# Graph attention's encoder on TensorE: exponentials as weights instead of values as weights

## The chip, the cores and the metric

The kernel runs on one core of a Trainium2 chip. A core has a matrix engine (TensorE: PE for its matmuls, PEld for its weight loads), VectorE (DVE), ScalarE (ACT), GpSimd (POOL) and SyncE (SP); the last two mostly issue transfers (DMAs). The matrix engine writes its results into eight PSUM banks, each of 512 float32 columns on 128 partitions. Everything else is held in SBUF or in the chip's main memory. The metric is the time of one whole execution in microseconds (us).

## What is computed

A stack of four graph layers on 2708 nodes with 512 features. The change lies in the first of them, an attention with 4 heads of 128 features each. The scores are a sigmoid of a sum of two numbers, one per target node and one per source node, and each head's weights are a softmax over a node's neighbours:

```python
Xw = einsum('hnd,hde->hne', Xh, W)
f1 = einsum('hnd,hd->hn', Xw, V[:, 0, :, 0])
f2 = einsum('hnd,hd->hn', Xw, V[:, 1, :, 0])
sig = sigmoid(f1[:, :, None] + f2[:, None, :])
att = softmax(where(adj != 0, adj * sig, -inf), axis=-1)
Xa = einsum('hij,hjd->hid', att, Xw)          # the encoder's attention
Xn = batchnorm(Xa); emb = batchnorm(elu(Xn @ We.T + be) + Xn)
Y = einsum('hij,hjd->hid', att, emb)          # the decoder's attention
```

Both patterns that the layer is given are the same matrix, so both softmaxes are one. After this layer come a graph convolution and two attention layers over the same matrix; the change doesn't touch them.

## The kernel before

The attention runs as a pass over parts. A part is one half of the target nodes (`hf`, 1354 nodes each) for two heads (`p`, heads 2p and 2p+1), in the order hf 0 p 0, hf 0 p 1, hf 1 p 0, hf 1 p 1. Within a part the loop at L465 goes over 22 blocks of source nodes, 21 of 128 and one of 20 (`ORDER` puts the short one in the middle).

For each block `form` (L367) makes the exponentials t, [source nodes, 2 heads, 1354 targets]:

- A load of the adjacency's block (`a`, four buffers) comes through SP's queue. In parts with p = 0 (`prepare`) VectorE turns its zeros into a large negative number (L396, L397), and GpSimd stores the result to `adj_d`. The parts with p = 1 read `adj_d` back.
- ScalarE takes a tanh for each head (L408), VectorE multiplies both by the block (L416), ScalarE takes the exponential of both (L417). t has four buffers.
- Some blocks' t (`kept_d`, 4 of a p = 0 part, 8 of a p = 1 part) are stored by GpSimd for the decoder (L486).

TensorE then multiplies (L504): the weights are the values `xw` of the block, 128 features of a head, and the exponentials stream through, 452 or 450 targets at a time. A part's results stand in six banks as [features, targets]: two heads by three chunks. A float32 matmul appears in the trace as two passes, each with its weight load.

The softmax's denominators are made by separate matmuls (L541): weights of 32 columns of ones, 340 targets at a time, four chunks in four column groups of the array, into the two banks `psm0` and `psm1`. In parts with p = 1 two neighbouring blocks are added on VectorE first (L531), so that one such set serves both; the first three and the last two blocks of a part stand alone.

At a part's end `keep` (L621) copies the six banks to `ft`, the features by nodes, on VectorE and ScalarE by turns. The denominators go to memory, come back spread over 80 partitions, are inverted there, go to memory again, and are loaded as a row on all partitions (`rb`). Results of the part are multiplied by it and counted for the batch norm (`bn_stats`) between the next part's blocks, one piece at a time from a list `later`. The last part does it at once with a matmul that spreads the reciprocals (L680). The decoder uses the reciprocals too, from `rs_d` in memory (`spread_sums`).

The order of each engine's instructions comes from a scheduler that places them by priorities and by its own times; each engine then works its list strictly in order. Waits between engines are semaphores. With the change, too, the order is fixed before the run.

Of the kernel before, what the change touches and what calls it, by code (L numbers as in the profile page):

```python
# [17 lines left out]
P = 128  # L18
# [11 lines left out]
def gnn_stack_kernel(  # L30
# [47 lines left out]
    ones = const.tile([P, P], F32, name="ones")  # L78
# [13 lines left out]
    def rows_tile(name):  # L92
        return big.tile([P, NT, F], F32, tag="rows", name=name)
# [52 lines left out]
    SQ = 4  # L146
    SW = 2 * ((HW + 2 * SQ - 1) // (2 * SQ))
    SCH = [[(q * SW, min(SW, w - q * SW)) for q in range(SQ)] for _, w in HSPAN]

# [8 lines left out]
    ALONE, LAST = 3, 2  # L158
    assert ORDER.index(NT - 1) % 2 == ALONE % 2 == NT % 2 + 1
# [18 lines left out]
    with ExitStack() as l0:  # L178
# [10 lines left out]
        SR = SQ * SW // 17  # L189
        assert SR <= P and SR * 17 == SQ * SW  # L190
        sum_d = dram.tile([H, NHALF, SQ, SW], F32, name="sum_d")
        rs_d = dram.tile([H, NHALF, SQ, SW], F32, name="rs_d")
# [4 lines left out]
        ones32 = p0.tile([P, 32], F32, name="ones32")  # L197
        nc.vector.memset(ones32, 1.0)
# [12 lines left out]
        xw = rows_tile("xw")  # L211
# [7 lines left out]
        def project(att, psum):  # L219
# [61 lines left out]
            def values_of(jt):  # L281
# [3 lines left out]
                for h in range(H):  # L285
# [10 lines left out]
                    xw[:n, jt, :].rearrange("p (a k d) -> p a k d", a=H // HP, k=HP),  # L296
# [13 lines left out]
            def rest(step):  # L310

                with tc.issue_after(step.ins):
# [7 lines left out]
                    copies(xw[:, NT - 1, :])  # L320
# [5 lines left out]
        def spread_sums(att, hf, p):  # L326

            w = HSPAN[hf][1]
            t = att.tile([P, HP, HW], F32, tag="rb", name="rb", bufs=1)
            src = rs_d[HP * p : HP * (p + 1), hf]  # L330
            even = (SQ - 1) * SW
            for k in range(HP):
                nc.sync.dma_start(
                    t[:, k, :even],
                    src[k, : SQ - 1].rearrange("r w -> (r w)").partition_broadcast(P),
                )
                nc.sync.dma_start(
                    t[:, k, even:w],
                    src[k, SQ - 1, SW - (w - even) :].partition_broadcast(P),
                )  # L340
            return t

        def attention_pass(values, first, att, psum, finish, f1b=None, blocks=(), spread=None, rest=None, taken={}):
# [84 lines left out]
            def sum_tiles():  # L428
                return [
                    psum.tile([P, BANK], F32, tag=f"psm{k}", name="psm", bufs=1) for k in range(HP)  # L430
                ]
# [4 lines left out]
            po = None  # L436
            for hf, (h0, w) in enumerate(HSPAN):
                for p in range(H // HP):
# [22 lines left out]
                    sums = None  # L461
                    if first and rest is None:
                        sums = sum_tiles()
                    before = None
                    for place, jt in enumerate(ORDER):  # L465
# [8 lines left out]
                        if kept is None or first:  # L474
# [6 lines left out]
                            if rest is not None:  # L481
                                rest(step)
                                rest = None
                                sums = sum_tiles()
# [7 lines left out]
                        if po is None:  # L492
# [6 lines left out]
                            po = [both[q][:, k, :] for k in range(HP) for q in range(HB)]  # L499
                        for k in range(HP):  # L500
# [10 lines left out]
                        if not first:  # L511
                            continue


                        if prepare or not ALONE <= place < NT - LAST:
                            whole, m = [t[:, k, :] for k in range(HP)], n
                        elif n < P:
                            m = P
                            for k in range(HP):
                                nc.vector.tensor_tensor(  # L520
                                    whole[k][:n, :w], whole[k][:n, :w], tv[:, k, :], ALU.add
                                )
                        elif before is None:
                            before = t
                            continue
                        else:

                            whole, m = [], P
                            for k, tag in enumerate(("z", "pair")):
                                both = att.tile([P, HW], F32, tag=tag, name="pair", bufs=1)  # L530
                                nc.vector.tensor_tensor(  # L531
                                    both[:, :w], before[:, k, :w], tv[:, k, :], ALU.add
                                )
                                whole.append(both)
                            before = None
                            if BLOCKS[ORDER[place + 1]][1] < P:
                                continue
                        for k in range(HP):
                            for r, (q0, qw) in enumerate(SCH[hf]):

                                nc.tensor.matmul(  # L541
                                    sums[k][32 * r : 32 * r + 32, :SW],
                                    ones32[:m],
                                    whole[k][:m, q0 + qw - SW : q0 + qw],
                                    start=(place == 0),
                                    stop=(place == NT - 1),
                                )
                    later += finish(hf, p, po, sums if first else rb) or []
# [20 lines left out]
        def stats_tile(name, k):  # L569
            return p0.tile([P, C, k, 6], F32, tag=name, name=name)  # L570
# [39 lines left out]
        stats = stats_tile("stats_a", SQ * NHALF)  # L610
        bias = p0.tile([P, 2, C], F32, name="enc_bias")
        with (
# [8 lines left out]
            def keep(hf, p, po, sums):  # L621
# [3 lines left out]
                final = hf == NHALF - 1 and p == H // HP - 1  # L625
                for k in range(HP):
                    for q, (q0, qw) in enumerate(HCH[hf]):
                        copy = nc.scalar.copy if q % 2 else nc.vector.tensor_copy
                        taken[q % 2] = copy(
                            ft[:, HP * p + k, h0 + q0 : h0 + q0 + qw], po[HB * k + q][:, :qw]  # L630
                        )
                sm = [att.tile([P, BW], F32, tag="rs", name="sm") for _ in range(HP)]
                if not final:
                    for k in range(HP):
                        h = HP * p + k
                        nc.vector.tensor_scalar(
                            sm[k][:, :SW], sums[k][:, :SW], TINY, None, ALU.max
                        )
                        nc.gpsimd.dma_start(sum_d[h, hf], sm[k][0 : 32 * SQ : 32, :SW])
                    part = slice(HP * p, HP * (p + 1)), hf  # L640
                    few = att.tile([SR, HP, 17], F32, tag="few", name="few", bufs=1)
                    wide = "h r w -> h (r w)"
                    cut = "h (s e) -> s h e"
                    nc.sync.dma_start(few, sum_d[part].rearrange(wide).rearrange(cut, s=SR))
                    nc.vector.reciprocal(few, few)
                    nc.sync.dma_start(rs_d[part].rearrange(wide).rearrange(cut, s=SR), few)
# [1423 lines left out]
```

## Time and profile before

| | us |
|---|---|
| median of 3 runs | 3197.55 (3196.16 to 3198.11) |
| the profiled execution's own time | 3195.56 |
| its span, first to last instruction | 3193.5 |
| encoder's attention, first to last matmul | 39.2 to 536.9 |
| granted TensorE clock, mean of the span | 0.997 |

In the four parts of the encoder's attention, and in the stage after it up to the encoder's MLP, the engines were busy as follows (us, instructions in brackets):

```profile
39.00:169.70 130.70, 130.12 (x621) 55.99 (x617) 119.09 (x73) 114.44 (x70) 18.11 (x32) 1.00 0.79 276
169.70:287.30 117.60, 116.58 (x474) 52.91 (x474) 104.68 (x66) 109.97 (x68) 6.24 (x11) 1.00 0.71 243
287.30:419.40 132.10, 131.13 (x617) 56.58 (x617) 122.08 (x88) 115.97 (x70) 15.21 (x27) 0.99 0.79 278
419.40:536.90 117.50, 116.56 (x476) 52.81 (x472) 96.45 (x68) 100.79 (x62) 4.95 (x9) 1.00 0.58 203
536.90:571.20 34.30, 31.34 (x109) 14.22 (x109) 25.93 (x41) 22.18 (x24) 5.59 (x8) 1.00 0.62 224
```

The columns are: the window and its length, then busy time of PE, PEld, DVE, ACT and POOL, the granted clock as a share of full speed, the mean busy share of the DMA engines, and what they moved in GB/s. Busy time counts each instruction to its end, although the next one on the same engine often starts a little earlier; the period from start to start is what tells how fast a sequence can go.

### The profile page before, as it was taken

What the parts mean: (1) busy time and instruction counts of PE and PEld (TensorE: products, weight loads), DVE (VectorE), ACT (ScalarE), POOL (GpSimd) and SP (SyncE); (2) the same over time, 40 slices, a digit from 0 to 9 for tenths busy, and PEclk for the clock granted to TensorE, in tenths of its full rate; (3) what the DMA queues carried; (4) which work ended last, traced back from release to release, by engine and by line L of the source; (5) the groups of instructions that cost most, each with busy time, mean ns of one, the idle gap of its engine ahead of it and who ended that gap; (6) DMA issues with size and microseconds to landing.
All of it is one profiled execution on the core that took longest, in us unless ns stands there. A gap on an engine that the chain in (4) does not pass through costs nothing.

```text
span 3193.5 us, 36039 instructions
## 1 busy us (share of the span) xinstructions
PE 3145.5 (98%) x13400; PEld 2125.6 (67%) x13400; DVE 2102.4 (66%) x3746; ACT 1356.7 (42%) x1623; POOL 202.7 (6%) x296
## 2 busy tenths in 40 slices
PE   8999999999999999999999999999999999999999
PEld 5444444544444446885578787777678888888886
DVE  7889987777686684444267667777644555555565
ACT  6899896477867552001133333434301111111111
POOL 1100100000000000000011111120110000000000
PEclk9999999999999999999999999999999999999999
DMA  7867875146555413541154445556431111111111
GB/s 274 314 223 251 284 246 188 65 155 236 173 167 199 172 61 98 144 125 43 40 149 138 140 143 150 154 174 177 132 102 36 52 50 49 49 52 50 49 45 34
DMA packets 207301, 429.81 MB, mean 135 GB/s; under 512 B 21966, under 2 KB 137474, under 8 KB 201302
## 3 DMA queue, kind: packets, MB, share of 16 engines
q1 hardware_dynamic: 183390, 324.15, 33.4%
q0 software_dynamic: 23296, 101.26, 8.5%
q8 instruction: 105, 1.72, 0.2%
q10 hardware_dynamic: 440, 2.10, 0.2%
q14 instruction: 70, 0.57, 0.1%
HBM read 330.07 MB, written 95.90 MB: 133 GB/s over the span
## 4 chain that ended last, share of the span: by engine, by line
PE 85%; DVE 6%; issue 3%; ACT 3%; DMA 2%; POOL 0%; SPq 0%; DVEq 0%; ACTq 0%; POOLq 0%
PE po L504 22%; PE po L1546 18%; PE ps_s L1342 17%; PE ps_nb L1156 7%; PE ps_wide L1206 5%; PE psm L541 3%; PE ps_sup L1734 2%; PE ps_mlp L792 2%; PE ps_hid L128 2%; PE ps_dec L923 2%; PE ps_v L128 1%; DVE t L416 1%; ACT t L408 1%; ACT t L417 1%; DVE e L1832 1%
## 5 line engine op out<-in xcount | busy, mean ns | idle before, releaser
L416 DVE SCALAR_TENSOR_TENSOR t<-t,a 128x2708 f32<-128x2708 f32 (+1 forms) x152 | 450.2, 2975 | 144.3 <-ACT t L408 140.3
L408 ACT ACTIVATE t<-f1b,f2h 128x1354 f32<-128x1354 f32 (+1 forms) x304 | 416.2, 1412 | 45.4 <-PE po L504 35.1
L417 ACT ACTIVATE t<-t 128x2708 f32<-128x2708 f32 (+1 forms) x152 | 373.1, 2456 | 98.8 <-DVE t L416 98.6
L504 PE MATMUL po<-t,xw 128*128 128x452 f32 (+3 forms) x1056 | 409.1, 551 | 3.5 <-ACT t L417 2.9
L1342 PE MATMUL ps_s<-q,hT 128*128 128x256 f32 (+1 forms) x1848 | 405.5, 372 | 0.0
L504 PE MATMUL po<-t,emb 128*128 128x452 f32 (+3 forms) x1056 | 397.6, 545 | 4.0 <-ACT t L417 3.8
L1546 PE MATMUL po<-sup,e 128*128 128x256 f32 (+1 forms) x1512 | 396.9, 384 | 3.1 <-DVE c L1627 2.1
L1342 PEld LDWEIGHTS ps_s<-q,hT 128*128 128x128 f32 x1848 | 339.2, 190 | 49.5 <-issue 6.4
L504 PEld LDWEIGHTS po<-t,xw 128*128 128x128 f32 (+1 forms) x1056 | 189.0, 190 | 211.8 <-issue 194.7
L504 PEld LDWEIGHTS po<-t,emb 128*128 128x128 f32 (+1 forms) x1056 | 193.5, 190 | 201.3 <-issue 190.8
L1546 PEld LDWEIGHTS po<-sup,e 128*128 128x128 f32 (+1 forms) x1512 | 264.2, 185 | 59.3 <-issue 21.5
L1546 PE MATMUL po<-held,T 128*128 128x256 f32 x1200 | 294.8, 380 | 4.8 <-DVE T L1503 4.8
L1546 PEld LDWEIGHTS po<-held,T 128*128 128x128 f32 x1200 | 226.3, 190 | 38.9 <-DVE T L1503 7.6
L1922 DVE SCALAR_TENSOR_TENSOR e<-a_cols,ps_s 128x512 f32<-128x512 f32 (+1 forms) x121 | 79.9, 660 | 238.1 <-PE ps_s L1342 231.9
L1342 PE MATMUL ps_s<-hT 128*128 128x256 f32 (+2 forms) x968 | 217.0, 375 | 4.3 <-DVE e L1832 3.4
L1342 PEld LDWEIGHTS ps_s<-hT 128*128 128x128 f32 x968 | 176.2, 192 | 32.7 <-DVE e L1832 3.8
L1828 ACT ACTIVATE a_score<-a_score,neg_big 128x512 f32<-128x512 f32 (+2 forms) x131 | 88.9, 686 | 256.6 <-DMA a_score<-in_adjT_dram 108.1
L1156 PE MATMUL ps_nb<-hid_hi,at 128*128 128x512 f32 x484 | 185.5, 390 | 0.4 <-DVE at L1148 0.4
L1156 PE MATMUL ps_nb<-hid_lo,at 128*128 128x512 f32 x462 | 180.0, 390 | 0.0
L1452 ACT ACTIVATE e<-e 128x512 f32<-128x512 f32 (+1 forms) x187 | 113.6, 617 | 133.2 <-DVE e L1451 130.1
L1914 ACT ACTIVATE q<-ps_wide,uq 128x256 f32<-128x256 f32 (+1 forms) x44 | 20.5, 467 | 337.1 <-PE ps_wide L1206 337.1
L1503 DVE TENSOR_TENSOR T<-e 128x256 f32<-128x256 f32 x200 | 84.2, 421 | 120.2 <-PE po L1546 97.1
(283 smaller groups left out, 4091.1 us busy)
## 6 DMA issues: line engine op xcount, KB each, us to landing
a<-adj_d SPq DMA_DIRECT2D x108, 677.0 KB
a_cols<-in_adjT_dram SPq DMA_DIRECT2D x200, 256.0 KB
a<-in_adjT_dram SPq DMA_DIRECT2D x42, 677.0 KB
adj_d<-a POOLq DMA_DIRECT2D x42, 677.0 KB, 5.3
kept<-t POOLq DMA_DIRECT2D x20, 1354.0 KB, 6.1
t<-kept SPq DMA_DIRECT2D x20, 1354.0 KB
raw<-in_adjT_dram SPq DMA_DIRECT2D x105, 256.0 KB
a_score<-in_adjT_dram SPq DMA_DIRECT2D x55, 256.0 KB
```

The costliest lines, as they stand in the source:

```text
L128: nc.tensor.matmul(ps[:n], xt[:, c, :n], w[:, c, :], start=(c == 0), stop=(c == C - 1))
L408: tanh = nc.scalar.activation(tv[:, k, :], f1b[k][:n, :w], AF.Tanh, bias=f2h[:n, jt, h : h + 1], scale=0.5,)
L416: step = nc.vector.scalar_tensor_tensor(tv, tv, GUARD, ab, ALU.add, ALU.mult)
L417: exp = nc.scalar.activation(tv, tv, AF.Exp, scale=0.5)
L504: nc.tensor.matmul(po[HB * k + q][:, :qw], values[r : r + n, jt, h * P : (h + 1) * P], t[r : r + n, k, q0 : q0 + qw], start=(place == 0), ...
L541: nc.tensor.matmul(sums[k][32 * r : 32 * r + 32, :SW], ones32[:m], whole[k][:m, q0 + qw - SW : q0 + qw], start=(place == 0), stop=(place = ...
L1156: nc.tensor.matmul(pos[it][:n], at, half[:, jt, :], start=(jt == 0 and k == 0), stop=(jt == NT - 1),)
L1206: nc.tensor.matmul(ps[:, :width], w(c, o), xt(c), start=(c == 0), stop=(c == C - 1),)
L1342: nc.tensor.matmul(ps[:, jb, i:w], keys[:, c, j : j + P], st["q"][:, c, i:], start=(c == 0), stop=(c == C - 1),)
L1452: nc.scalar.activation(e, e, AF.Exp)
L1546: nc.tensor.matmul(po[bank][rows, half, :], lhsT, rhs, start=(k == 0 and half == 0) if first is None else first, stop=last, skip_group_che ...
L1828: nc.scalar.activation(a, a, AF.Identity, bias=neg_big[: a.shape[0]], scale=1.0e30)
```

## The change

In the encoder's attention the roles of the two operands are exchanged. A block of exponentials, 128 sources by 128 targets, is loaded as weights, and the values stream through it, 128 features and a column of ones: 129 columns. The result is [targets, features], with the denominator in its last column. A half has 11 groups of targets (10 of 128 and one of 74). Three results of 129 columns fit a bank, so each of the two heads takes four banks, and all eight are in use. The matmuls of `ones` and the pair sums are no longer there.

At a part's end VectorE takes each group's denominators (maximum with a tiny number, reciprocal) and multiplies the results out of PSUM into `rows`. TensorE turns `rows` back to [features, targets] by transposes, into banks of the part's second head, and VectorE copies these to `ft`. This (`turn`) is issued during the next part's first two blocks, one head in each; the second head's matmuls of these two blocks are held back (`waiting`) until then. The reciprocals are turned as well and stored to `rs_d`. The decoder's pass keeps its form, and reads the reciprocals as one row.

```diff
-    ones = const.tile([P, P], F32, name="ones")
+    ones = const.tile([P, 1], F32, name="ones")
...
+    VW = F + H
...
-        xw = rows_tile("xw")
+        xw = rows_tile("xw", VW).rearrange("p t (h e) -> p t h e", h=H)
+        nc.vector.memset(xw[:, :, :, P:], 1.0)
...
-            for k in range(HP):
-                nc.sync.dma_start(
-                    t[:, k, :even],
-                    src[k, : SQ - 1].rearrange("r w -> (r w)").partition_broadcast(P),
-                )
-                nc.sync.dma_start(
-                    t[:, k, even:w],
-                    src[k, SQ - 1, SW - (w - even) :].partition_broadcast(P),
-                )
+            for k in range(HP):
+                nc.sync.dma_start(
+                    t[:, k, :w], rs_d[HP * p + k, h0 : h0 + w].partition_broadcast(P)
+                )
...
+            def node_sums(k, place, jt, t, w, hf):
+                n = BLOCKS[jt][1]
+                slots = list(range(NB))
+                if n < P:
+                    slots.sort(key=lambda r: r % PER)
+                for r in slots:
+                    b, s = divmod(r, PER)
+                    i0, m = NODES[hf][r]
+                    own = 0 if n == P else b % HB * Q
+                    nc.tensor.matmul(
+                        po[k][b][:m, s * DR : (s + 1) * DR],
+                        t[own : own + n, k, i0 : i0 + m],
+                        values[own : own + n, jt, HP * pair + k, :],
+                        start=(place == 0 and s == 0),
+                        stop=(place == NT - 1),
+                        skip_group_check=True,
+                    )
...
+                        if first:
+                            node_sums(0, place, jt, t, w, hf)
+                            waiting.append(lambda a=(1, place, jt, t, w, hf): node_sums(*a))
+                            if turns:
+                                turns.pop(0)()
+                            if not turns:
+                                for work in waiting:
+                                    work()
+                                waiting = []
+                            continue
...
-                        if prepare or not ALONE <= place < NT - LAST:
-                            whole, m = [t[:, k, :] for k in range(HP)], n
...
-                                nc.tensor.matmul(
-                                    sums[k][32 * r : 32 * r + 32, :SW],
-                                    ones32[:m],
-                                    whole[k][:m, q0 + qw - SW : q0 + qw],
-                                    start=(place == 0),
-                                    stop=(place == NT - 1),
-                                )
...
-            def keep(hf, p, po, sums):
+            def keep(hf, p, po, later):
...
+                for k in range(HP):
+                    rc = att.tile([P, NB], F32, tag="rc", name="rc", bufs=4)
+                    nc.vector.memset(rc[:, NB - 1 :], 1.0)
+                    rows = att.tile([P, NB, P], F32, tag="rows", name="rows")
...
+                    for b, g in groups:
+                        m = NODES[hf][g[0]][1]
+                        src = po[k][b][:m, g[0] % PER * DR : (g[-1] % PER + 1) * DR]
+                        src = src.rearrange("p (r e) -> p r e", e=DR)
+                        own = rc[:m, g[0] : g[-1] + 1]
+                        nc.vector.tensor_scalar(own, src[:, :, P], TINY, None, ALU.max)
+                        nc.vector.reciprocal(own, own)
+                        taken[k] = nc.vector.tensor_tensor(
+                            rows[:m, g[0] : g[-1] + 1, :],
+                            src[:, :, :P],
+                            own.unsqueeze(2).to_broadcast([m, len(g), P]),
+                            ALU.mult,
+                        )
...
+                def turn(k):
+                    h = HP * p + k
+                    rows, rc = kept[k]
+                    for b in range(TURNS):
+                        slots = range(b * QUAD, min(NB, (b + 1) * QUAD))
+                        bank = po[1][(TURNS * k + b) % (HB + 1)]
+                        for r in slots:
+                            i0, m = NODES[hf][r]
+                            nc.tensor.transpose(
+                                bank[:, r % QUAD * P : r % QUAD * P + m],
+                                rows[:m, r, :],
+                                ident[:m, :m],
+                            )
...
+                        if b + 1 == TURNS:
+                            nc.tensor.transpose(bank[:NB, BANK - P :], rc, ident)
+                            sm = att.tile([NB, P], F32, tag="sm", name="sm")
+                            nc.vector.tensor_copy(sm, bank[:NB, BANK - P :])
...
+                        nc.vector.tensor_copy(dst, bank[:, :cw])
+                        later.append(
+                            lambda dst=dst, n=TURNS * hf + b: nc.vector.bn_stats(
+                                stats[:, h, n, :], dst
+                            )
+                        )
...
-                    nc.tensor.matmul(pm, ones, w1_held[:, c, :], start=(c == 0), stop=(c == C - 1))
+                    nc.tensor.matmul(pm, ones.to_broadcast([P, P]), w1_held[:, c, :], start=(c == 0), stop=(c == C - 1))
```

## The prediction

> **What bounds the kernel now.** I read the page first (busy shares and the chain), then the busy time by stage inside the encoder's attention, then the timelines of VectorE, ScalarE and TensorE there.
>
> ```profile
> span 3193.5 us, 36039 instructions
> PE 3145.5 (98%) x13400; PEld 2125.6 (67%) x13400; DVE 2102.4 (66%) x3746; ACT 1356.7 (42%) x1623; POOL 202.7 (6%) x296
> ...
> PE po L504 22%; PE po L1546 18%; PE ps_s L1342 17%; PE ps_nb L1156 7%; PE ps_wide L1206 5%; PE psm L541 3%; PE ps_sup L1734 2%; PE ps_mlp L792 2%; PE ps_hid L128 2%; PE ps_dec L923 2%; PE ps_v L128 1%; DVE t L416 1%; ACT t L408 1%; ACT t L417 1%; DVE e L1832 1%
> ```
>
> The chain runs along TensorE. Only the encoder's half of L504 and all of L541 (the sums, 3%) belong to this change.
>
> ```profile
> core 0: us, PE busy (x) PEld busy (x) DVE busy (x) ACT busy (x) POOL busy (x), PEclk, DMA share, GB/s
> 109.00:170.00 61.00, 61.00 (x289) 26.44 (x282) 51.42 (x33) 52.27 (x33) 6.42 (x11) 1.00 0.82 288
> 437.00:530.00 93.00, 92.07 (x360) 42.27 (x356) 81.66 (x57) 82.94 (x50) 3.77 (x7) 1.00 0.61 217
> ```
>
> TensorE is full in both kinds of part, but VectorE and ScalarE stand at 84 to 89%. A gain on TensorE is soon capped, so I need the period of each engine for one block of 128 sources.
>
> The chain of waits, in order of time (start, us; two blocks of the first part), and then the timelines of VectorE and ScalarE there:
>
> ```profile
> 115.45 4.75 PE po L504 x12
> 121.48 4.75 PE po L504 x12
> ```
>
> ```profile
> 62.42 2.98 DVE L416 SCALAR_TENSOR_TENSOR t<-t,a 128x2708 f32<-128x2708 f32 x1
> 65.32 0.86 DVE L396 TENSOR_SCALAR z<-a 128x1354 f32<-128x1354 f32 x1
> 66.22 1.57 DVE L397 SCALAR_TENSOR_TENSOR a<-z,a 128x1354 f32<-128x1354 f32 x1
> 67.92 2.98 DVE L416 SCALAR_TENSOR_TENSOR t<-t,a 128x2708 f32<-128x2708 f32 x1
> ```
>
> ```profile
> 57.65 2.73 ACT L408 ACTIVATE t<-f1b,f2h 128x1354 f32<-128x1354 f32 x2
> 60.27 2.44 ACT L417 ACTIVATE t<-t 128x2708 f32<-128x2708 f32 x1
> 62.62 1.41 ACT L408 ACTIVATE t<-f1b,f2h 128x1354 f32<-128x1354 f32 x1
> ```
>
> From start to start: TensorE 6.03 us (chain of waits; 12 passes and then the sums), VectorE 5.50 us in a preparing part (two heads, p=0), ScalarE 62.62-57.65 = 4.97 us. In the p=1 parts VectorE has only the 2.9 us product plus pair sums, and TensorE's pair of blocks repeats every 10.58 us in the chain, 5.29 a block. The chain puts the four parts at 39.2, 169.7, 287.3 and 419.4, and the last sum's end at 536.9 us: 130.5, 117.6, 132.1, 117.5 us.
>
> [...] the projections at L286 (130 columns, new 128-column weights for each pass) advance by 30 passes between these two windows, (5.60-2.24)/30 = 112 ns, with weight loading busy all the time.
>
> ```profile
> 22.00:24.24 2.24, 2.24 (x23) 2.24 (x22) 1.00 0.84 300
> 22.00:27.60 5.60, 5.60 (x53) 5.60 (x52) 1.00 0.93 271
> ```
>
> [...] the 452-column copy at L629 takes 620 ns here [...]. [...] Outputs at multiples of 129 words start at odd words; no row here shows one.
>
> **The change, part by part.**
>
> TensorE. Gone per block: 12 passes of 0.379 (the 4.75 us rows are 12 with the tail) = 4.55 us and the sums, 6.03-4.55 = 1.48 alone or 0.74 a block in pairs. Added: 11 node groups x 2 heads x 2 passes = 44 passes of 129 columns. Nearest row L286: 44 x 0.112 = 4.93 us. The bounds of a pass are 109 ns (128-column transposes are paced so) [...]; I take 112. Each part adds 24 transposes, 24 x 0.11 = 2.6 us. Had TensorE alone counted, the encoder would lose some 55 us; it doesn't.
>
> Preparing parts. VectorE's 5.50 us a block is not touched and now comes last (TensorE 4.93, ScalarE 4.97). The order of ScalarE leaves slack: a block's exponential needs VectorE's product, the next tanh comes in between. Part 1: the row at 62.42 is the sixth block's product; the 22nd starts 16 x 5.50 later, at 150.4; plus 2.9 (product), 2.4 (exponential), 4.9 (TensorE) = 160.6 instead of 169.7: **-9 us**. Before, VectorE ran ahead and TensorE trailed by two blocks.
>
> p=1 parts. Gone from VectorE: 16 pair adds x 1.5 = 24 us, which lay beside TensorE. Now ScalarE 4.97 against TensorE 4.93; ScalarE alternates two exponentials and four tanhs, and with four t buffers the second tanh pair needs the block before last free, which leaves about 1 us. So 5.29 (6.03 for six blocks or so) becomes 4.97: 22 x 4.97 = 109.3. The stores of kept t at POOL take 5.8 us to land against 4.9 on TensorE, so a buffer can be up to 1 us late in half of the eight cases: 0 to 4 us a part, and 0 taken, since the slack is as large.
>
> The hand-over between parts is new. Before: 4 copies on VectorE, 2 on ScalarE, and TensorE went on as each bank came free. Now VectorE makes per part 10 maxima and 10 reciprocals of 1 to 3 columns (0.15 us as f2h at L299, or 0.2 where one waits for the other, partly interleaved: 0.12 on average = 2.4), 6 products of 384 (0.47 by the 340-column product at L688, 0.51, less overlap) and 4 of 128 (0.21): together 6.1 us. Then transposes go into the second head's own banks, and VectorE copies them: 4 x 0.62 + 2 x 0.42 + 2 x 0.15 = 3.6 us. Six bn_stats cost 3.3 us. Together 13 us, before 10.3 (2.2 copies, 0.9 maxima, 8 x 0.43 products, 8 x 0.43 bn_stats, 0.3). The second head's matmuls of the first two blocks wait for all of that, and VectorE's order places the products of blocks 2 and 3 of the new part among the scalings. Following it by hand from the end of a preparing part (time 0): first head scaled +1.5, second head and product 2 +7, copies 1 and product 3 +12.5, copies 2 +14.5; the second head of blocks 1 and 2 ends at +19.5 and block 4 at about +27.5, where four undisturbed blocks need 19.7. So a hole of **8 us**; p=1 parts become 27.5 + 18 x 4.97 = 117 against 117.6 and 117.5, **-0.5** each. The gain in the steady part is given back at its start.
>
> Part 3 starts with VectorE's 13 us of hand-over and then 22 x 5.50, less two preparations (5 us) that move into part 2's end, plus some 4 us until TensorE has caught up: 133 against 132.1, **+1**. VectorE was nearly the bound there before, too (22 x 5.50 + 10.3 = 131).
>
> End. From the last sum to the scale of the batch norm, 536.9 to 550.3, before: 12 us of VectorE with two 340-column reciprocals (4.4 us for both). After: 13 us less what lies beside TensorE's last head, no such reciprocals, but the products and the copies of one head more in a row: -1.5 to +1, taken -0.5. The next load of rb waits for the store of the reciprocals in both.
>
> Edits at nothing: ones narrowed, broadcast as weights for four matmuls; the memset of xw's ones column under the first loads; xw's copies at stride 129; two rb loads in place of four; SP loses six small transfers and POOL gets 16 short ones for 8, behind which stores of adj_d wait a few us (four a-buffers cover that; uncovered, one 6 us wait). From the encoder's MLP on, TensorE's order is the same.
>
> Sum: -9 - 0.5 + 1 - 0.5 - 0.5 (the end) = -9.5. The profiled execution's own time is 3195.56 (span 3193.5 plus 2.1); it lies 2.0 below the median of the runs, 3197.55. On that median: 3188.
>
> **Rivals.** (a) The hand-over hides: t's four buffers let ScalarE run on, and scaling costs 4 us. Then p=1 parts are 112 and the total -20: 3178. For it: VectorE is idle half of a p=1 part. Against: the products stand among the scalings in its fixed order.
> (b) Holes of 12 to 13 us in place of 8, and as much again at part 3: gain of part 1 used up, 3198. For it: dependent small operations at 0.2 us each would add 2 us per part, and each PSUM bank goes TensorE-VectorE-TensorE-VectorE.
> (c) Slower: [...] Then TensorE needs 5.5 us a block: nothing in the preparing parts, 22 x 0.53 = 12 us in each p=1 part, total +15: 3212. It decides from about 117 ns on (10 us over 2 x 22 x 44 passes is 5 ns). For it: L541 streamed rows through few weights, now every pass loads full weights, with no reserve. Against: L286 and its 112 ns.
> (d) The sums' passes aren't removed: excluded, no L541 is left in the changed order.
>
> **How the numbers follow.** Forecast 0.54 (3180 to 3194), (a) 0.12, (b) 0.14, (c) 0.20. No change is within 0.2%, 3191 to 3204, about what this measurement can tell. Faster: 0.50 of the forecast and (a), 0.62; same: the forecast's rest and most of (b), 0.17; slower: (c) and a little of (b), 0.21. The range 3174 to 3206 leaves out the far ends of (a) and (c); the forecast's own is 3180 to 3194.
>
> **What would show it.** Passes to po at 110 to 113 ns and a first preparing part that ends near 161 us; VectorE at 5.50 us a block and almost always busy there; in p=1 parts ScalarE starting a block every 4.97 us; holes in TensorE of 8 us or so at each start, with the second head's matmuls waiting for copies to ft; the last matmul to po near 527. A pass near 120 ns, a preparing part with VectorE waiting for loads, or holes over 12 us would prove it wrong.

## The result

The change made the kernel slower. Five runs of each on the same chip gave 3210.67 us (3204.93 to 3214.98) after and 3198.11 us (3196.16 to 3200.32) before: a ratio of 1.0038, 95% interval 1.0023 to 1.0052, or 12.6 us. The forecast was 3188 us, and the measured time also lies above its range (3174 to 3206). The profiled execution of the changed kernel is the quickest of its five, 3204.93 us; against the 3195.56 us of the profile before it shows 9.4 us of the difference.

The top of the page, with the share of each line in the chain that ended last:

```profile
span 3203.1 us, 39602 instructions
PE 3107.7 (97%) x15176; PEld 2353.6 (73%) x15176; DVE 2052.1 (64%) x3797; ACT 1350.0 (42%) x1615; POOL 203.6 (6%) x304
...
PE po L1537 18%; PE ps_s L1333 17%; PE po L530 10%; PE ps_nb L1147 7%; PE ps_wide L1197 5%; PE ps_hid L131 2%; PE ps_sup L1725 2%; PE ps_mlp L783 2%; PE po L433 2%; PE ps_dec L914 2%; PE ps_v L131 1%; ACT t L412 1%; DVE t L411 1%; ACT t L403 1%; DMA kept<-t 1%
```

TensorE and VectorE are both less busy than before (by 38 and 50 us), and the kernel is longer. Before, the encoder's matmuls and sums held the chain; now L433, which does the same work, holds 2% of it, and the last entry is a transfer that the list before does not have: the store of kept exponentials. TensorE now waits for others.

The busy times by stage, the four parts and then the stage up to the encoder's MLP (same columns as before):

```profile
39.00:167.80 128.80, 114.43 (x969) 111.67 (x969) 115.89 (x81) 109.72 (x67) 16.94 (x30) 0.95 0.79 275
167.80:288.30 120.50, 111.26 (x975) 109.24 (x974) 79.55 (x60) 110.19 (x67) 7.33 (x14) 0.97 0.66 227
288.30:424.00 135.70, 119.99 (x1016) 116.94 (x1015) 126.52 (x122) 111.77 (x67) 15.59 (x28) 0.95 0.73 259
424.00:543.40 119.40, 110.00 (x994) 108.06 (x992) 74.29 (x68) 102.34 (x61) 6.28 (x12) 1.00 0.56 195
543.40:579.40 36.00, 30.30 (x105) 13.94 (x103) 22.13 (x49) 20.05 (x23) 3.81 (x7) 0.86 0.53 191
```

Part 1 became 1.9 us shorter (130.7 before), the other three 2 to 4 us longer (117.6, 132.1, 117.5 before). The encoder's last matmul ends at 543.3 us instead of 536.7 (here and below its end is the point at which a next pass could start; the modelled end, 536.9 before, is some 0.15 us later). From there to the first matmul of the MLP (`ps_mlp`) it takes 36.1 us instead of 31.8. Both together are the loss: the first `ps_mlp` starts at 579.4 instead of 568.5, and what follows takes 2623.7 us after and 2625.0 before. Compared instruction by instruction on VectorE, the distance between the two runs stays near 11 us (10.1 to 12.3) from 611 to 1720 us; later it wanders by a few us, in these two and in all other runs of this study.

What was forecast for the steady state came in. VectorE in a preparing part, and TensorE and ScalarE in part 2 (timelines: start, duration; "x125" is a run of 125 passes in one row):

```profile
62.24 2.98 DVE L411 SCALAR_TENSOR_TENSOR t<-t,a 128x2708 f32<-128x2708 f32 x1
65.13 0.86 DVE L391 TENSOR_SCALAR z<-a 128x1354 f32<-128x1354 f32 x1
66.03 1.57 DVE L392 SCALAR_TENSOR_TENSOR a<-z,a 128x1354 f32<-128x1354 f32 x1
67.73 2.98 DVE L411 SCALAR_TENSOR_TENSOR t<-t,a 128x2708 f32<-128x2708 f32 x1
```

```profile
204.78 14.10 PE L433 MATMUL po<-xw,t 128*128 128x129 f32 x125
...
239.36 4.79 ACT L412 ACTIVATE t<-t 128x2708 f32<-128x2708 f32 x2
244.06 5.36 ACT L403 ACTIVATE t<-f1b,f2h 128x1354 f32<-128x1354 f32 x4
249.32 4.80 ACT L412 ACTIVATE t<-t 128x2708 f32<-128x2708 f32 x2
254.02 5.36 ACT L403 ACTIVATE t<-f1b,f2h 128x1354 f32<-128x1354 f32 x4
259.28 4.79 ACT L412 ACTIVATE t<-t 128x2708 f32<-128x2708 f32 x2
```

VectorE starts a product every 5.49 us, ScalarE a pair of blocks every 9.96 us (4.98 a block), and passes of 129 columns follow each other at 111 to 112 ns (14.10 us less the 0.27 of the last pass, over 124 steps), which is 4.9 us for the 44 passes of a block. So the loss is not in the rates. It is in waits, and the profile lists them. First the waits of ScalarE and then those of TensorE in the encoder of the changed kernel, last those of TensorE before:

```profile
ACT t L403 <- DMA kept<-t: 25.2, 9, 5.7
ACT t L412 <- DVE t L411: 24.6, 15, 6.2
ACT t L403 <- PE po L433: 10.5, 11, 2.6
...
ACT t L403 <- DMA f1b<-f_d: 4.0, 2, 3.8
```

```profile
PE po L433 <- ACT t L412: 39.0, 28, 4.3
PE po L433 <- DVE rows L636: 5.3, 4, 1.7
PE po L433 <- DVE rc L634: 3.6, 1, 3.6
```

```profile
PE po L504 <- ACT t L417: 2.9, 3, 1.0
```

TensorE waits 39 us for ScalarE's exponentials, 2.9 us before. Part of that is an engine that is simply ahead of its supplier. But ScalarE itself waits 25.2 us, nine times, for a transfer `kept<-t`: a tanh wants to write a t buffer whose exponentials are still being stored. Before, the list of ScalarE's waits has no such row. Of the 25.2 us, 16.1 lie in the two p=0 parts (four waits) and 9.1 in the p=1 parts (five waits). The longest, in part 1, and two of part 2:

```profile
95.44 1.43 ACT L403 ACTIVATE t<-f1b,f2h 128x1354 f32<-128x1354 f32 x1 [5.74 <-DMA kept<-t]
...
206.23 4.79 ACT L412 ACTIVATE t<-t 128x2708 f32<-128x2708 f32 x2
210.93 4.04 ACT L403 ACTIVATE t<-f1b,f2h 128x1354 f32<-128x1354 f32 x3
217.19 1.43 ACT L403 ACTIVATE t<-f1b,f2h 84x1354 f32<-84x1354 f32 x1 [2.23 <-DMA kept<-t]
...
228.07 1.43 ACT L403 ACTIVATE t<-f1b,f2h 128x1354 f32<-128x1354 f32 x1 [0.80 <-DMA kept<-t]
```

In the p=1 parts, the fourth tanh after a pair of exponentials goes into the buffer of the first one of that pair. Worked out on the undisturbed pair at 239.36: the first exponential ends near 241.8, the fourth tanh starts at 244.06 + 3 x 1.31 = 248.0, which is 6.2 us later; the buffer of the second one is due only 11.2 us after its exponential, at 255.3. A store of a whole block takes 7.3 us in the median to land (6.1 before), and from 4.9 to 10.9 in the encoder. So in these parts a block that is stored from the first place of a pair can make ScalarE wait (five of six did, for 0.8 to 3.1 us), and no block from the second place did. ScalarE at 4.98 us a block and TensorE at 4.9 have no reserve to make such a wait good.

Before, ScalarE's order was looser. The block of the row at 206.23, the first of its pair, is made at 200.27 there, and the next tanh into its buffer is the second one of the row at 213.40:

```profile
200.27 2.44 ACT L417 ACTIVATE t<-t 128x2708 f32<-128x2708 f32 x1
...
213.40 4.04 ACT L408 ACTIVATE t<-f1b,f2h 128x1354 f32<-128x1354 f32 x3
```

That is 12.0 us after the exponential's end (213.40 + 1.31 - 202.71). Read in this way, no whole block that was stored in the p=1 parts before was due sooner than 10.4 us.

### The profile page after: what moved, and what is told of

Read it like the earlier page. It is cut to its first block, busy times and chain, and to the rows that moved or that the text cites. A ratio compares the mean times of both kernels' runs of the same rounds, so it can differ in the third digit from the quotient of the medians.

```text
span 3203.1 us, 39602 instructions
## 1 busy us (share of the span) xinstructions
PE 3107.7 (97%) x15176; PEld 2353.6 (73%) x15176; DVE 2052.1 (64%) x3797; ACT 1350.0 (42%) x1615; POOL 203.6 (6%) x304
## 4 chain that ended last, share of the span: by engine, by line
PE 72%; issue 11%; DVE 7%; DMA 5%; ACT 3%; POOL 1%; SPq 0%; DVEq 0%; POOLq 0%; ACTq 0%
PE po L1537 18%; PE ps_s L1333 17%; PE po L530 10%; PE ps_nb L1147 7%; PE ps_wide L1197 5%; PE ps_hid L131 2%; PE ps_sup L1725 2%; PE ps_mlp L783 2%; PE po L433 2%; PE ps_dec L914 2%; PE ps_v L131 1%; ACT t L412 1%; DVE t L411 1%; ACT t L403 1%; DMA kept<-t 1%
## 5 line engine op out<-in xcount | busy, mean ns | idle before, releaser
L433 PE MATMUL po<-xw,t 128*128 128x129 f32 (+2 forms) x3872 | 448.5, 282 | 48.7 <-ACT t L412 39.0
L433 PEld LDWEIGHTS po<-xw,t 128*128 128x128 f32 (+2 forms) x3872 | 438.1, 192 | 59.2 <-ACT t L412 50.1
```

Source lines behind the costliest of these rows:

```text
L433: nc.tensor.matmul(po[k][b][:m, s * DR : (s + 1) * DR], t[own : own + n, k, i0 : i0 + m], values[own : own + n, jt, HP * pair + k, :], sta ...
```

## The experiments

Ten kernels ran. Where an experiment has several timed runs, its median stands beside the median of the kernel before in the same series (3195.5 to 3197.2 us), and the difference between them is what is compared: the changed kernel's is +12.6 us, from the series of the result; it was not timed again beside the experiments. "Encoder's end" is the end of its last matmul in the profiled run, 543.3 after and 536.7 before.

**No stores of t, in both kernels.** One edit, once in the changed kernel and once in the kernel before. The decoder then makes all its exponentials anew, about 40 us more work; so not the total is compared, but the encoder alone.

```diff
-    KEPT = [(8, 11, 14, 18), (1, 4, 7, 9, 11, 14, 17, 20)]
+    KEPT = [(), ()]
```

> The changed kernel with no t stored for the decoder (the decoder's pass then makes all of its exponentials again, so only the time up to the encoder's last matmul to po is read; it was 543.4 us in the profile after). Theory A (the buffers of t are held by the stores of kept t, ScalarE then waits, TensorE idles and its clock is halved for some us): the 25 us of ScalarE's waits for these stores go, the half-clock windows in the encoder fall from 9 to 3 or fewer, and the last matmul to po comes at 525 to 533. Rival B (the hand-over between the parts is what costs; the stores are hidden): it stays at 539 or later.

> The same left out of the kernel before, as the control. A and B both: its encoder is bound by TensorE, so the last sum stays at 537, 1 us off at most. Were it to come 5 us earlier or more, the stores would have cost there, too, and A's gain would be no cause of the difference between the two kernels.

Measured: 3230.05 us for the changed kernel without stores and 3235.66 us for the kernel before without them, one run each. The encoder's end moved from 543.3 to 525.4 us in the changed kernel, and from 536.7 to 538.2 in the kernel before. Leaving out the same stores brings the encoder's end 17.9 us forward in one kernel and not at all in the other. ScalarE's waits in the changed kernel without them:

```profile
ACT t L412 <- DVE t L411: 33.7, 34, 7.1
ACT t L403 <- PE po L433: 8.6, 11, 2.2
```

Neither `kept` nor `f1b` is left in the list, and the encoder ends 1.6 us before the forecast's 527. This shows that the stores, with what hangs on them, are the main cause. The 17.9 us are not the stores' waits alone, though: the wait for `f1b` (the next experiment) goes with them, and the scheduler's order is another one, with the pairs of p=1 parts beginning at even places instead of odd ones. What theory A of this run had wrong: TensorE's time at half clock (see below) hardly fell with the waits, to 44 us from 48 within the first 900 us (in the encoder to 27 from 34). So most of these stretches are not made by the stores, and the encoder ends in time in spite of them.

**The load of f1b ahead of a part's last exponential: two ways to take it away.** The other row of ScalarE's waits, `f1b`, is short but lies at a bad place. ScalarE's timeline at the end of part 1:

```profile
147.90 0.35 ACTq L464 DMA_DIRECT2D f1b<-f_d  x1
...
159.04 1.43 ACT L403 ACTIVATE t<-f1b,f2h 128x1354 f32<-128x1354 f32 x1 [3.84 <-DMA f1b<-f_d]
160.37 2.44 ACT L412 ACTIVATE t<-t 128x2708 f32<-128x2708 f32 x1
```

The exponential at 160.37 is the last one of part 1; two tanhs of part 2's first block stand ahead of it, and the second waits for its row of f1, whose load could be issued only at 147.90, after the last tanh out of that buffer, and took 11.1 us. Before, the scheduler had one tanh there, then the exponential, then the other tanh. The first experiment changes the order alone, the second gives f1b a fourth buffer (and `f1c`, which lives before the attention, one in place of two, for the room).

```diff
+                exps.append(exp)
...
+                                if first and place == 0 and exps:
+                                    order.enter_context(tc.issue_after(exps[-1].ins))
```

> The changed kernel; the tanhs of a part's first block are kept behind the exponential of the part before on ScalarE, so that this exponential no longer waits for the load of the second f1b row. A (with the f1b load as its second place): the last exponentials of parts 1 and 3 come 5 to 6 us earlier (160.4 to 155, 416.3 to 411), the encoder's end moves from 543.4 to 533 to 537, the time falls by 6 to 10 us to about 3202. Rival B: these exponentials come earlier but the hand-over absorbs it, the end moves by less than 3 us.

```diff
-    att.tile([P, HW], F32, tag="f1b", name=name, bufs=HP + 1)
+    att.tile([P, HW], F32, tag="f1b", name=name, bufs=HP + 2)
```

> The changed kernel with a fourth f1b buffer (and one f1c buffer in place of two), so that the second row can be loaded ahead in most parts. A: as in the run with the order changed, 4 to 10 us faster than the changed kernel, about 3202. B: within 3 us of the changed kernel.

Measured: order 3208.67 us, +12.0 against the kernel before; fourth buffer 3206.89 us, +10.3. In the profiled runs part 1's last exponential started at 153.8 and 156.7 in place of 160.4, and the encoder's end moved by -4.3 and -5.1 us (539.0 and 538.2). So the load is a second cause, worth 4 to 5 us of the encoder in the profiles; of that, 0.6 and 2.3 us show in the medians, fewer than expected (6 to 10 and 4 to 10) and within their own uncertainty of about 4 us (the intervals of the ratios, 1.0022 to 1.0047 and 1.0021 to 1.0047, overlap that of the changed kernel). So in the whole time this cause is not shown. ScalarE still waited 24.8 and 18.3 us for stores.

**Stores at other places.** If it is the place and not the number of stores that counts, then moving those of p=1 to the second block of each pair must take their waits away.

```diff
-    KEPT = [(8, 11, 14, 18), (1, 4, 7, 9, 11, 14, 17, 20)]
+    KEPT = [(8, 11, 14, 18), (2, 4, 6, 8, 12, 14, 16, 18)]
```

> The changed kernel, with the stored places of the p=1 parts moved from 1, 4, 7, 9, 11, 14, 17, 20 to 2, 4, 6, 8, 12, 14, 16, 18; the number of stores is the same. Theory A (a store holds ScalarE only where the next tanh into the same buffer is due sooner than the store's 7.3 us): in the p=1 parts the exponential of an odd place is the first of its pair and its buffer is due again 6.2 us after it, that of an even place 11.2 us after it. So the waits of p=1 parts for stored t (7, 9, 11, 17: about 9 of the 25.2 us in all) go, those of the p=0 parts (8 and 14) stay: some 16 us of waits in all, the encoder's last matmul about 5 us earlier (538), first ps_mlp 574, total 3206. Rival (the waits are a matter of how many bytes are stored, and move along with the stores): waits stay near 25 us, the encoder's last matmul at 543, total 3210.

Measured: 3202.17 us, +6.7. ScalarE's waits for stores fell from 25.2 us to

```profile
ACT t L403 <- DMA kept<-t: 15.7, 5, 6.0
```

as expected, all of them in p=0 parts, and the encoder's end came 6.5 us earlier, at 536.8. But the profiled run, the slowest of its five (3210.78 us), lost 7 us again in the decoder. Its second part has no longer a stored block at place 1, and TensorE waited for the exponential that ScalarE now makes there (timeline of TensorE):

```profile
754.57 3.57 PE L530 MATMUL po<-t,emb 128*128 128x452 f32 x9
763.90 7.07 PE L530 MATMUL po<-t,emb 128*128 128x452 f32 x12 [5.75 <-ACT t L412]
```

The set of places is shared by the encoder, where a store costs, and the decoder, where a load helps.

**The stage after the encoder.** There the chain of waits of the changed kernel runs (start, duration):

```profile
550.47 0.67 PE tp_w L710 x4
...
553.59 1.13 PE tp_w L710 x4
...
556.99 10.76 DMA rb<-rs_d
```

`tp_w` are transposes of two weight matrices in eight groups, which use `psm0` and `psm1` by turns. Before, both were free for them once the sums had been read. Now the second head's first transposes go to `psm1` and hold it until 550.4. The scheduler pulled the four groups of `psm0` ahead, and the four of `psm1` are left to go one after another, each waiting for ScalarE's copy. By the chain, the decoder's load of f1b, and of rb behind it on SP's queue, waits for ScalarE's `bn_scale` (L111), which stands behind seven of the eight copies: it starts 13.3 us after the encoder's end, 11.6 before. The edit lets the second head's transposes use the three banks that the first head's use, and leaves `psm1` to only two of the eight groups.

```diff
-                        bank = po[1][(TURNS * k + b) % (HB + 1)]
+                        bank = po[1][b]
...
-                    slot = o % 2
+                    slot = k * (o % 2)
```

> The changed kernel, with nothing but the encoder's end changed: the second head's transposes use the three banks of po[1] that the first head's used (not the single bank psm1 for its first group), and of the eight groups of weight transposes (tp_w) after the encoder only wk's second and fourth use psm1, the others psm0. Theory T (the tail is longer because four tp_w groups with psm1 wait for the second head's first transposes, then go one after another at 1.79 us each, and the loads of f1b and rb for the decoder wait for the last of them): SP's f1b load comes about 10 us after the encoder's last matmul in place of 13.1, first ps_mlp 32 to 33 us after it in place of 36.1, total 3207. Rival (the halved clock and 3.7 MB of loads and stores that share the DMA engines set the tail): first ps_mlp stays 35 to 36 us after the last matmul, total 3210.

Measured: 3201.46 us (19 runs), +6.0. In the profile the first `ps_mlp` comes 28.4 us after the encoder's end in place of 36.1, more than the 3 to 4 us expected. TensorE's timelines say where the 7.7 us are, first the changed kernel, then this one:

```profile
557.37 5.98 PE L726 MATMUL ps_m<-emb 128*128 128x512 f32 x8 [0.87 <-ACT emb L715]
563.28 3.59 PE L589 MATMUL ps_shift<-enc_w,bn_shift 128*1 128x512 f32 x8
```

```profile
553.60 3.70 PE L726 MATMUL ps_m<-emb 128*128 128x512 f32 x8 [0.68 <-ACT emb L715]
557.23 3.59 PE L589 MATMUL ps_shift<-enc_w,bn_shift 128*1 128x512 f32 x8
```

The first `ps_m` starts 9.5 us after the encoder's end (544.1 here) in place of 14.1: 4.6 us. Its eight passes take 3.70 us and not 5.98, as the clock stays at 1.00 in the whole stage: 2.3 us. And VectorE copies `ps_shift` (L592) as soon as it is made, while in the changed kernel, as in the one before, `linked` (L862), which waits for rb, stood ahead of it:

```profile
568.07 0.87 DVE L862 TENSOR_SCALAR linked<-rb 128x1354 bf16<-128x1354 f32 x1 [1.53 <-DMA rb<-rs_d]
568.85 0.67 DVE L592 COPY emb<-ps_shift 1x512 f32<-1x512 f32 x1
```

`ps_shift` was made at 566.9 there (563.28 + 3.59), so this cost 2.0 us. The sum is 8.8 (before rounding), of which 1.1 is lost again between the copy and `ps_mlp`. The loads of f1b and rb start 9.9 us after the encoder's end and not 13.3. rb still lands some 10 us after its first load is issued, as in the changed kernel (10.8; 8.1 before), so that the rival is right on the transfers, but with the copy ahead TensorE no longer waits for rb. Of the 7.7 us, 6.1 are left by 590 us (compared on VectorE): TensorE waits 0.8 us for the copy of `ps_u`, which has come to stand behind the decoder's first products on VectorE. In the versions below with these banks the lead at the first `ps_mlp` shrinks by 3 us in the same stretch. Which of the three terms came from the banks and which from the scheduler's new order was not taken apart.

**All together.** The fourth f1b buffer, the places of the fifth experiment and the banks of the sixth:

> The changed kernel with three edits together: four f1b buffers (as in e4), the stores of p=1 at even places (as in e5), the banks of the encoder's end (as in e6). If the three causes are apart from each other: encoder's last matmul 543.3 - 5 - 5 = 533, first ps_mlp 565.5 to 566, some 14 us before the changed kernel's, total 3197, about level with the kernel before. If they overlap, as waits of one engine one after another do: encoder's last matmul 537, first ps_mlp 570, total 3202.

Measured: 3199.37 us, +3.9. The encoder's end is at 529.1 us, 14.2 earlier than in the changed kernel, and the first `ps_mlp` at 557.5, 11 us before the kernel before reaches it. So the causes add up, and by more than expected (533). But of the lead that is left at 590 us all 8 us are lost again in the decoder at the same place as above.

Then the stores of p=0 were moved as well, those of p=1 to odd places, because with this set the pairs begin at even ones:

```diff
-    KEPT = [(8, 11, 14, 18), (2, 4, 6, 8, 12, 14, 16, 18)]
+    KEPT = [(0, 2, 12, 20), (3, 5, 7, 9, 13, 15, 17, 19)]
```

> As e7, with the stores of the p=0 parts moved too, from places 8, 11, 14, 18 to 0, 2, 12, 20, where the next tanh into the buffer is due 7 us or more after the exponential, and those of p=1 at 3, 5, 7, 9, 13, 15, 17, 19, since with this set the exponential of an even place comes first in its pair. Theory A: hardly a wait for stored t remains (under 6 us), encoder's last matmul 527 to 530, first ps_mlp 559 to 562; total 3191 to 3194 if the decoder loses nothing by its loads' places. Rival 1 (what holds the encoder is the hand-over and TensorE's idle gaps): encoder's last matmul stays at 533 or later. Rival 2: the decoder, whose loads of stored exponentials now lie closer together at the start of a p=0 part, gives 3 us or more back; then the time after first ps_mlp is 2628 or more in place of 2624 to 2625.

Measured: 3211.04 us, +15.5: a miss, and both rivals were right. The waits for stores fell only to 10.5 us, ScalarE now waited 18.3 us for TensorE (8.4 of it in one piece, at part 3's start), the encoder's end came at 538.2, and the time after the first `ps_mlp` grew to 2644 us. A set of places is also an input to the scheduler's order: here it put an exponential of the next part's first block ahead of the last one of parts 1 and 3, which it does in no other kernel of this study. Which part of the loss is due to that was not followed further.

**The best version.** So only those p=1 places move that are first in their pair, and place 1 stays:

```diff
-    KEPT = [(8, 11, 14, 18), (1, 4, 7, 9, 11, 14, 17, 20)]
+    KEPT = [(8, 11, 14, 18), (1, 4, 6, 8, 12, 14, 18, 20)]
```

> As e7 (four f1b buffers, the banks of the encoder's end, p=0 stores at 8, 11, 14, 18), but the p=1 stores at 1, 4, 6, 8, 12, 14, 18, 20: only those places are moved whose buffer was due again 6.2 us after the exponential (7 to 6, 9 to 8, 11 to 12, 17 to 18). In e7 the decoder made good 8 us of the encoder's gain where its second part has no stored block at place 1: TensorE waited 5.75 us there for ScalarE. Theory A, with the decoder's place 1 kept: encoder's last matmul 529 to 531, first ps_mlp 557 to 560, and the offset to the kernel before still -8 to -10 us after the decoder: total 3187 to 3191, ratio to before 0.997 to 0.999. Rival (the decoder or the stages behind it take the lead back whatever is loaded, since transfers or the decoder's own bound set the time): 3195 to 3200, level with before.

> Four f1b buffers and the banks of the encoder's end, with the stores where the changed kernel has them. Theory A: the encoder's last matmul as in e4 (538), first ps_mlp 28.4 us later as in e6 (566.5), 2 us before the kernel before; total 3194 to 3198; the difference to e9, 7 to 8 us, is what the stores of the p=1 parts cost by themselves. If the stores' waits were only shifted by the f1b buffers, e9 and this run end within 2 us of each other.

Measured, in one series: with the places moved 3189.86 us (17 runs), -7.4 against 3197.22, a ratio of 0.9977 (0.9969 to 0.9985); with f1b and banks alone 3201.85 us (13 runs), +4.6, ratio 1.0014 (1.0005 to 1.0022). The encoder's ends are 532.9 and 540.7 (expected 529 to 531, and 538), the first `ps_mlp` 561.3 and 569.1: each some 2 to 3 us late, and the second version's time is above the expected 3194 to 3198. The difference between the two is 7.8 us in the profiles, as expected; in the medians it is 12.0. Four stores of each p=1 part, moved by one place, decide between slower and faster than the kernel before. ScalarE's waits in the better one:

```profile
ACT t L412 <- DVE t L411: 35.3, 22, 5.6
ACT t L403 <- DMA kept<-t: 13.9, 6, 3.6
```

The profiled run of the better version is among its slow ones (3196.26 us, third from the top of 17). It is 7.2 us ahead of the profile before at the first `ps_mlp` and some 5 us from 860 to 1600 us; by 2450 us it has lost that, in stages that the change does not touch. So the trace shows the gain up to there, and only the medians show that it lasts to the end.

The changed kernel with these three side effects mended (what is left in the p=0 parts stays) is 0.2% faster than the kernel before, where the change alone is 0.4% slower.

## Why the prediction was wrong

- **The step that failed** is the cost of the stores of kept t: "0 to 4 us a part, and 0 taken, since the slack is as large" in the p=1 parts, and no cost at all in the p=0 parts. ScalarE waited for them 5.3 and 3.8 us in the two p=1 parts and 16.1 us in the two p=0 parts, and without them the encoder ends 17.9 us earlier. In the p=1 parts the pattern was right, and so was "half of the eight cases": the first block of a pair has 6.2 us, the other 11.2. Too small was the landing. The 5.8 us are the median of all 24 stores in the trace of before, four of which hold the short block only; whole blocks took 6.1 us there and 7.3 in the changed kernel, and 5.1 to 9.0 at the places in question (7, 9 and 17). Of the 20 stores of a whole block in the encoder (1354 KB each) only four landed in 4.9 to 5.0 us; the other 16 took 5.1 to 10.9, with the DMA engines at 0.56 to 0.79 of their time.
- **In p=0 parts** a buffer is due again 5.3 to 5.4 us after its exponential at places 6 to 11 (in the run without stores), and the longest wait, 5.74 us at 95.44, belongs to place 8 of part 1. So part 1's -9 us became -1.9. Without stores the last product of part 1 starts at 150.5 us and TensorE's last pass ends at 162.0, where the forecast put 150.4 and 160.6: VectorE's 5.50 us as the bound was right. What these stores cost by themselves was not tested; moving those of p=1 brought the encoder's end 6.5 and 7.8 us forward, so a good part of the 17.9 is theirs or that of f1b.
- **The load of f1b** was left out. It costs 4 to 5 us in the encoder, by the profiles.
- **The end** was taken as -0.5 and was +4.3. The working followed VectorE, whose share came out even shorter than forecast (its last step before the scale, L110, starts 10.8 us after the encoder's end, 13.4 before), and did not follow the banks `psm0` and `psm1` to their next user, the weight transposes, and the loads behind these.
- **The hand-over** of 8 us was slightly too large. Without stores TensorE has done the first four blocks of the p=1 parts 24.9 and 26.5 us after the part before, where 27.5 was forecast and 19.7 would be undisturbed: holes of 5.2 and 6.8 us, between rival (a)'s 4 and the forecast's 8. The steps that the forecast gave VectorE there came in: in the changed kernel a product of 384 columns takes 0.47 us from start to start and one of 128 columns 0.20 (0.47 and 0.21 forecast), the copies out of the transposes' banks 0.60 and 0.41 (0.62 and 0.42). The parts take 115.3 and 116.5 us from last pass to last pass, where 117 was forecast. Rival (b), larger holes, is refuted.
- **The pass** of 129 columns takes 111 to 112 ns, with outputs at odd columns among them; rival (c), the case held for slower (TensorE at 5.5 us a block), is refuted as well. Its longer pass was an estimate of the author's that no trace showed, and so the chance of slower stood on the wrong cause. Part 3 came out nearly as forecast: 131.8 us from last pass to last pass without stores, 133 forecast.
- All in all the encoder's own sum was right to 2 us, part by part, for a kernel whose exponentials nobody stores. The error was to leave a cost at its value of before, while the change took away what had paid for it: before, the buffers of the stored whole blocks in p=1 parts were due after 10.4 us or more, now after 6.2 at a pair's first place. How much of that comes from TensorE's pace (5.29 us a block, which left ScalarE 0.3 us) and how much from the scheduler's new order of ScalarE was not taken apart.

**TensorE's clock.** The forecast said nothing of it, and it is still open what it costs. In windows over the stage after the encoder (columns as before, the third number from the end is the clock):

```profile
542.00:551.80 9.80, 7.11 (x58) 5.85 (x57) 9.71 (x35) 2.93 (x5) 1.92 (x4) 1.00 0.01 3
551.80:562.00 10.20, 7.98 (x18) 4.20 (x19) 3.04 (x11) 3.13 (x5) 1.41 (x3) 0.50 0.50 136
562.00:570.00 8.00, 7.21 (x20) 1.97 (x18) 2.42 (x4) 6.14 (x7) 0.00 (x0) 1.00 1.00 406
```

The clock is at half for 10.24 us. In the 9.8 us before, at full clock, TensorE did 58 passes and was busy for 7.11 us. The first eight passes of `ps_m` take 5.98 us, the first 4.6 of them at half clock, against 3.67 in the kernel before, at full clock: 2.3 us. In the encoder of the changed kernel nine such stretches add up to 34 us, one of 3.4 us before. As the run without stores ended in time with 27 us of them in its encoder, they are not the main loss; what they take from the other versions was not measured.

## What to carry to other kernels

When a change takes the bound off one engine, list every transfer that holds a buffer and compare, block by block, the time until that buffer is due again with the time until the transfer lands; a mean slack hides that one block of a pair has half as much as the other. Follow a scratch buffer or PSUM bank that the change newly uses to its next user, also past the end of the changed loop. And where the same list of places serves two stages, move a place only if it is paid for in both.

## What the runs showed of the hardware that was not expected

- In the profiles before and after, the half-clock stretches last 3.41, 6.83 or 10.24 us, once, twice or three times the shortest, but for the one that runs past the end of the span. What sets them off was not tested. Before the one at 551.8 TensorE's longest gap since the encoder's end is 1.0 us, and in the last 3.41 us TensorE was busy for 1.68.
- A store of 1354 KB took from 4.9 to 10.9 us to land in the same kernel, and one of them, in a preparing part with the DMA engines at 0.79 of their time, held ScalarE 5.74 us.
- The run-to-run spread of the whole kernel grew: 16.1 us over the 17 runs of the best version, 8.9 us over the 29 runs of the kernel before beside them. Where it comes from is open. In the profiled runs the distance to the kernel before wanders by up to 7 us between 1700 and 2450 us, in stages that the change does not touch.
